# An attention and quantized-FFN kernel on one core: the last group of the up projection stays on chip for the down projection, and the general path becomes loops

## The chip, the cores and the metric

The kernel runs on one core of one Trainium2 chip. A core has TensorE (PE in the profile; its weight loads are PEld), VectorE (DVE), ScalarE (ACT), GpSimd (POOL) and SyncE (SP), which here issues almost all DMAs. The metric is the device time of one execution in microseconds, the median over several executions.

## The reference

The input x is (2, 2048, 512), ctx is (2, 128, 512). The kernel computes

```python
x = x + xattn(layernorm(x), ctx, Wq, Wkv)       # softmax attention, 128 keys
x = x + ffn(layernorm(x), w_gate, w_up, w_down) # 512 -> 1536 -> 512

def ffn(x, w_gate, w_up, w_down):
    x = act_qdq(x)
    up = act_qdq(x @ lpbq_dequant(w_up).T)
    gate = act_qdq(x @ lpbq_dequant(w_gate).T)
    sig = fixed_qdq_u16(sigmoid(gate))
    gate = act_qdq(gate * sig)
    o = act_qdq(gate * up)
    return o @ lpbq_dequant(w_down).T
```

`act_qdq` rounds a whole tensor to 16-bit integers with one scale, max|v| / 32767. `lpbq_dequant` rounds weights to 4 bits in blocks of 32. Every scale is a maximum over a whole tensor, so a stage can't round its result before all of it is known. The 16-bit integers are split into parts of at most 12 bits, and one product becomes three fp32r products: two summed in a PSUM tile q, the third in e.

## The kernel before

The 4096 tokens are 8 groups of 512. The 1536 features of the FFN are 12 chunks of 128, taken as 3 tiles of 4 chunks. The kernel has these stages in a row: attention and layernorm; gate (all groups, 0 to 7); up (groups 7 down to 0); down; the store of the last rows.

**Up** is the loop L688–742. For each of 24 (group, tile) pairs j and each of two halves (half tile c = 2j + h), `project` (L502–511) makes 24 matmuls into q and e. ACT evicts q (L709), DVE subtracts e (L710), SP stores the half tile of u to DRAM (`up_d`, L717). Beside this, `next_gelu` (L591–599) reads a gate tile j + 2 ahead (1 MB, `load_gate`, two buffers) and lets ACT make its integers gi, the sigmoid sig in a tile of its own, and its 16-bit integers sq. `integers_of_p` (L651–658) multiplies gi and sq on DVE to the integers p and stores them (`p_d`). `bound` (L660–664) lets ACT take |u| (L662) and DVE the maximum of |u| p (L663, `pumax`). `umax` collects the maxima of |u|. At the start of group 0, `load_step(0)` (L629, L638, L640) loads what the first step of down needs: p of 256 tokens as 6 DMAs of 128 KB, u as 6 DMAs of 256 KB, x1 as 512 KB; this is read from group 7, since down goes through groups 7 to 0. In group 0 each of the three tiles also issues the loads of four weight chunks of down without their third part (512 KB each, L738); the twelve third parts (256 KB each) follow at L742.

**Between up and down** the scale of o has to be found. `fetch_best` (L668–686) finds for each partition the half tile whose |u| p is greatest, makes a row index on DVE (L674) and lets POOL read that row of u and of p back from DRAM with indirect DMAs (L679). The last half tile isn't among them and is treated from SBUF. L745–751 make r_u, the reciprocal scale of u, over all partitions (with a transpose by TensorE). L757 rounds the last half tile and the fetched rows on ACT, L758 takes the maximum of the product on DVE, L763 the maximum over partitions on POOL. L818–821 make a flag that tells whether this maximum is sure to be the greatest; L823 reads the flag into a register of every engine, and L824 branches. If the flag is 0 a **general path** (L825–862) reads all gate, u and p tiles again; it is written out 24 + 24 times. It isn't entered with these inputs, and all engines jump over it.

**Down** (L865–895) has 16 steps of 256 tokens, each of two units of 128. A step loads the next step's p, u and x1 (`load_step`), rounds u on ACT (`round_up`, L776), and for each unit makes the parts of o (`round_o`: DVE L790, L791, L793, L795, ACT cast L792), 24 matmuls into q (L881), 12 into e (L885), and finishes with ACT (L889), POOL (L891), DVE (L893) and a store (L895). The first unit's parts are made in three pieces.

The order of instructions on each engine comes from the tile framework's scheduler, that of the source lines with priorities; every engine works its own list in order and waits by semaphores. SP issues its DMAs in its own order too, so one that waits holds the ones behind it.

Of the kernel before, what the change touches and what calls it, by code (L numbers as in the profile page):

```python
# [63 lines left out]
P = 128  # L64
# [12 lines left out]
def tile_xattn_ffn(  # L77
# [39 lines left out]
    x1_d = dram.tile([NG, P, NJ, D], F32, name="x1_d")  # L117
    gate_d = dram.tile([NG * NK, P, NQ, TG], F32, name="gate_d")

# [36 lines left out]

    def abs_max(col, src, axis=AX.X):
        nc.vector.tensor_reduce(col, src, axis, ALU.max, apply_absolute_value=True)
# [75 lines left out]
    cp = ExitStack()  # L234
    with ExitStack() as c0:
# [254 lines left out]
        homes = [cp.enter_context(tc.tile_pool(name="parts0", bufs=1))]  # L490
# [22 lines left out]
        with ExitStack() as c2:  # L513
# [16 lines left out]
            homes.append(home1.__enter__())  # L530
# [7 lines left out]
            for t in range(NG):  # L538
# [8 lines left out]
                for k in range(NK):  # L547
# [13 lines left out]
                    nc.sync.dma_start(out=gate_d[n], in_=g4)  # L561
# [4 lines left out]
    order = [(t, k) for t in reversed(range(NG)) for k in range(NK)]  # L566
    with cp, ExitStack() as c3:
        gp2 = c3.enter_context(tc.tile_pool(name="gate", bufs=2))
        wk1 = c3.enter_context(tc.tile_pool(name="wkc1", bufs=1))
        wk2 = c3.enter_context(tc.tile_pool(name="wkc2", bufs=2))  # L570
        wk3 = c3.enter_context(tc.tile_pool(name="wkc3", bufs=3))
# [7 lines left out]
        def load_gate(t, k, queue=nc.sync):  # L579
            gt = gp2.tile([P, NQ, TG], F32, tag="gt", name=f"gt_{t}_{k}")  # L580
            queue.dma_start(out=gt, in_=gate_d[t * NK + k])
            return gt

        gts = [load_gate(*at, nc.gpsimd) for at in order[:2]]
# [6 lines left out]
        def gelu_like(pool, pool1, gt, shape, name):  # L591

            gi = pool.tile([P] + shape, I16, tag="gi", name=f"gi_{name}")
            nc.scalar.activation(gi, gt, AF.Copy, scale=r_g)
            sig = pool1.tile([P] + shape, F32, tag="sig", name=f"sig_{name}")
            nc.scalar.activation(sig, gi, AF.Sigmoid, scale=s_g)
            sq = pool.tile([P] + shape, U16, tag="sq", name=f"sq_{name}")
            nc.scalar.activation(sq, sig, AF.Copy, scale=65536.0)  # L598
            return gi, sq


        gi, sq = gelu_like(const, const, top_g, [1], "top")
# [13 lines left out]
        wd, ready, loaded = [], [], {}  # L616

        lds = []

        def where_of(t):  # L620


            g, i = divmod(t * TD, TG)
            return g, NG - 1 - g, i

        def load_p(t, v):
            g, _, i = where_of(t)
            for c in range(2 * NK):
                nc.sync.dma_start(out=v[:, ts(c, 2), :], in_=p_d[g * 2 * NK + c, :, :, ds(i, TD)])  # L629

        def load_step(t):
            g, tg, i = where_of(t)
            pool = lds[t % 2]
            pi = pool.tile([P, NF, TD], I16, tag="p5", name=f"p5_{t}")
            load_p(t, pi)
            uv = pool.tile([P, NF, TD], F32, tag="u5", name=f"u5_{t}")
            for c in range(2 * NK):
                nc.sync.dma_start(out=uv[:, ts(c, 2), :], in_=up_d[g * 2 * NK + c, :, :, ds(i, TD)])  # L638
            x1 = pool.tile([P, TD // P, D], F32, tag="x1", name=f"x1_{t}")
            nc.sync.dma_start(out=x1, in_=x1_d[tg, :, ds(i // P, TD // P), :])  # L640
            loaded[t] = pi, uv, x1

        def next_gelu():

            j = len(ready)
            if j < len(order):
                ready.append(gelu_like(wk3, wk1, gts.pop(0), [NQ, TG], j))
                if j + 2 < len(order):
                    gts.append(load_gate(*order[j + 2]))

        def integers_of_p(j):  # L651
            gi, sq = ready[j]
            pi = wk3.tile([P, NQ, TG], I16, tag="pi", name=f"pi_{j}")
# [6 lines left out]
        def bound(c, u, pi):  # L660
            ua = wk2.tile([P, 2, TG], F32, tag="ua", name=f"ua_{c}")
            nc.scalar.activation(ua, u, AF.Abs)  # L662
            nc.vector.tensor_tensor_reduce(ua, ua, pi, 1.0, 0.0, ALU.mult, ALU.max, pumax[:, c : c + 1])  # L663
            return ua

        best = const.tile([P, 8], F32, name="best")

        def fetch_best():  # L668
# [5 lines left out]
            nc.vector.scalar_tensor_tensor(row, where[:, 0:1], float(P), lane, ALU.mult, ALU.add)  # L674
# [11 lines left out]
            return fetched  # L686

        LAST = len(order) - 1  # L688
        for j, (t, k) in enumerate(order):
            if k == 0:  # L690
# [3 lines left out]
                if t == 0:  # L694
                    home1.__exit__(None, None, None)
                    lds.append(ctx.enter_context(tc.tile_pool(name="ld0", bufs=1, side="right")))
                    load_step(0)
            u4 = wk2.tile([P, NQ, TG], F32, tag="u4", name=f"u4_{j}")
            if j:
                pi = integers_of_p(j)  # L700
            for h in range(2):
                c = 2 * j + h
                both = slice(2 * h, 2 * h + 2)
                q = ps_m.tile([P, 2, TG], F32, tag="q", name=f"q_u{c}")
                e = ps_m.tile([P, 2, TG], F32, tag="e", name=f"e_u{c}")
                for i in range(2):
                    project(wu[NQ * k + 2 * h + i], parts, q[:, i, :], e[:, i, :])
                if c + 1 < NH:
                    nc.scalar.activation(u4[:, both, :], q, AF.Copy, scale=1.0 + 1.0 / BASE)  # L709
                    nc.vector.tensor_tensor(u4[:, both, :], u4[:, both, :], e, ALU.subtract)  # L710
                else:
                    for i in range(2):
                        v = u_last[:, i, :]
# [205 lines left out]
```

## Time and profile before

| | us |
|---|---|
| median of 5 runs | 1027.84 (1023.53 to 1030.06) |
| the profiled execution | 1027.78 |
| its span in the profile | 1026.0 |

One execution was profiled, at a mean granted TensorE clock of 0.967. Of its span, PE is busy 951.1 us (93%), PEld 765.5 (75%), DVE 801.1 (78%), ACT 541.8 (53%), POOL 81.1 (8%). The page cuts the span in 40 slices of 25.65 us; digits are tenths of a slice in which the engine was busy:

```profile
PE   6998875999999999997999999999549999999998
PEclk9999896999999999999999999999869999999999
DMA  9087644886895775897789988896978876666520
```

The first eight slices are attention, then gate, up from slice 18 on, and down from slice 29 to the end. The two slices near the middle of the right half with 5 and 4 on PE are the transition from up to down. The row PEclk is the clock that TensorE was granted. Costliest on DVE in up are the subtraction of e (57.2 us), L663 (57.3) and L654 (56.4), in down L790 (61.2).

### The profile page before, as it was taken

Reading aid. Unit: us, or ns where it says so; the run is one execution under the profiler, and the core shown is the slowest. Engines: PE = TensorE matmul, PEld = TensorE weight load, DVE = VectorE, ACT = ScalarE, POOL = GpSimd, SP = SyncE. Lnnn points to the kernel's source line nnn. Section 1 sums busy time; section 2 is a strip of 40 time slices with the busy share of each in tenths; the row PEclk is TensorE's granted clock in tenths of the full one; section 3 lists DMA queues with packets and bytes.
Section 4 is the critical chain, followed back from the end, with each engine's and each line's share of the span. In section 5 each row is a group of like instructions: output and inputs, shape, how many; then the busy total and the mean of one; then the engine's idle time right before and its main releaser. Section 6 shows DMA issues by size and latency. Waiting matters only on the chain. (4 is left out here: it accounts for less than half of the span.)

```text
span 1026.0 us, 11754 instructions
## 1 busy us (share of the span) xinstructions
PE 951.1 (93%) x4321; PEld 765.5 (75%) x4321; DVE 801.1 (78%) x969; ACT 541.8 (53%) x610; POOL 81.1 (8%) x67
## 2 busy tenths in 40 slices
PE   6998875999999999997999999999549999999998
PEld 5765643888888888876888888888338888888886
DVE  4489865899997989445898888788558997877882
ACT  2268786432333323219998898886335344344431
POOL 0101111000000000000000000000001321122111
PEclk9999896999999999999999999999869999999999
DMA  9087644886895775897789988896978876666520
GB/s 337 18 320 273 246 180 172 325 335 273 322 376 187 301 228 176 272 391 290 288 320 376 346 314 326 341 359 222 415 243 264 277 241 202 222 207 200 175 74 31
DMA packets 127262, 268.47 MB, mean 262 GB/s; under 512 B 7456, under 2 KB 75040, under 8 KB 118496
## 3 DMA queue, kind: packets, MB, share of 16 engines
q1 hardware_dynamic: 126160, 263.75, 71.3%
q0 software_dynamic: 512, 2.88, 0.8%
q10 hardware_dynamic: 528, 1.05, 0.3%
q8 instruction: 34, 0.56, 0.2%
q14 instruction: 28, 0.23, 0.1%
HBM read 140.77 MB, written 126.88 MB: 261 GB/s over the span
## 5 line engine op out<-in xcount | busy, mean ns | idle before, releaser
L881 PE MATMUL yq<-wd,parts_o 128*128 128x512 f32 x768 | 181.9, 393 | 24.1 <-DMA p<-p_d 24.1
L507 PE MATMUL q_g<-parts_g,wg 128*128 128x512 f32 x768 | 196.0, 396 | 5.1 <-ACT parts_g L225 5.1
L881 PEld LDWEIGHTS yq<-wd,parts_o 128*128 128x128 f32 x768 | 145.8, 190 | 55.0 <-ACT parts_o L792 24.3
L507 PEld LDWEIGHTS q_g<-parts_g,wg 128*128 128x128 f32 x768 | 144.4, 189 | 38.1 <-ACT parts_g L225 6.2
L555 ACT ACTIVATE g<-q_g 128x512 f32<-128x512 f32 x96 | 57.3, 599 | 183.0 <-PE q_g L507 178.7
L507 PE MATMUL q_u<-parts_u,wu 128*128 128x512 f32 x576 | 144.2, 392 | 0.0
L507 PEld LDWEIGHTS q_u<-parts_u,wu 128*128 128x128 f32 x576 | 108.1, 188 | 24.4
L511 PE MATMUL e_g<-parts_g,wg 128*128 128x512 f32 x384 | 106.3, 395 | 0.0
L556 DVE CUSTOM_DVE_ANT_0 g<-g,e_g 128x512 f32<-128x512 f32 x96 | 64.6, 679 | 39.0 <-PE e_g L511 38.5
L885 PE MATMUL ye<-wd,parts_o 128*128 128x512 f32 x384 | 92.2, 389 | 0.0
L511 PEld LDWEIGHTS e_g<-parts_g,wg 128*128 128x128 f32 x384 | 72.2, 189 | 15.7
L885 PEld LDWEIGHTS ye<-wd,parts_o 128*128 128x128 f32 x384 | 72.1, 188 | 15.0
L511 PE MATMUL e_u<-parts_u,wu 128*128 128x512 f32 x288 | 77.9, 392 | 0.0
L889 ACT ACTIVATE yqs<-yq,q_o 128x512 f32<-128x512 f32 x32 | 22.0, 687 | 100.9 <-PE yq L881 100.9
L792 ACT CAST parts_o<-sa_o 128x1536 fp32r<-128x1536 int16 (+1 forms) x34 | 47.4, 1397 | 48.7 <-PE ye L885 26.3
L891 POOL TENSOR_TENSOR qx<-yqs,x 128x512 f32<-128x512 f32 x32 | 55.1, 1723 | 217.6 <-ACT yqs L889 205.3
L663 DVE CUSTOM_DVE_ANT_0 ua<-ua,pi 128x1024 f32<-128x1024 f32 x47 | 57.3, 1221 | 18.8 <-ACT ua L662 18.6
L654 DVE SCALAR_TENSOR_TENSOR pi<-gi,k_p,sq 128x2048 int16<-128x2048 int16 x24 | 56.4, 2350 | 16.9 <-ACT sq L598 16.1
L790 DVE SCALAR_TENSOR_TENSOR oi<-p,k_o,ui 128x1536 int16<-128x1536 int16 (+1 forms) x34 | 61.2, 1808 | 9.3 <-DVEq L824 5.9
L710 DVE TENSOR_TENSOR u<-u,e_u 128x1024 f32<-128x1024 f32 x47 | 57.2, 1217 | 8.6 <-ACT u L709 8.6
L511 PEld LDWEIGHTS e_u<-parts_u,wu 128*128 128x128 f32 x288 | 54.1, 188 | 12.2
L893 DVE SCALAR_TENSOR_TENSOR y<-ye,e_o,qx 128x512 f32<-128x512 f32 x32 | 24.0, 750 | 47.2 <-PE ye L885 37.9
(178 smaller groups left out, 1415.8 us busy)
## 6 DMA issues: line engine op xcount, KB each, us to landing
gate_d<-g SPq DMA_DIRECT2D x24, 1024.0 KB, 6.5
u<-up_d SPq DMA_DIRECT2D x96, 256.0 KB, 4.7
up_d<-u SPq DMA_DIRECT2D x47, 512.0 KB, 6.3
gt<-gate_d SPq DMA_DIRECT2D x22, 1024.0 KB, 7.9
parts_d<-parts_g SPq DMA_DIRECT2D x6, 3072.0 KB, 11.4
parts_u<-parts_d SPq DMA_DIRECT2D x6, 3072.0 KB, 12.4
p_d<-pi SPq DMA_DIRECT2D x24, 512.0 KB, 9.7
p<-p_d SPq DMA_DIRECT2D x96, 128.0 KB, 2.9
```

Of the source, the lines that this page charges most:

```text
L507: nc.tensor.matmul(q, lhsT=w[:, s, c, :], rhs=parts[:, s, c, :], start=(c + s == 0), stop=(c + s == ND))
L511: nc.tensor.matmul(e, lhsT=w[:, 2, c, :], rhs=parts[:, 2, c, :], start=(c == 0), stop=(c == ND - 1))
L555: nc.scalar.activation(g4[:, i, :], q, AF.Copy, scale=1.0 + 1.0 / BASE)
L556: nc.vector.tensor_tensor_reduce(g4[:, i, :], g4[:, i, :], e, 1.0, LOWEST, ALU.subtract, ALU.max, gtop[:, m : m + 1])
L654: nc.vector.scalar_tensor_tensor(pi, gi, k_p, sq, ALU.mult, ALU.mult)
L663: nc.vector.tensor_tensor_reduce(ua, ua, pi, 1.0, 0.0, ALU.mult, ALU.max, pumax[:, c : c + 1])
L710: nc.vector.tensor_tensor(u4[:, both, :], u4[:, both, :], e, ALU.subtract)
L790: nc.vector.scalar_tensor_tensor(oi[:, c], pi[:, c], k_o, ui[:, c], ALU.mult, ALU.mult)
L792: nc.scalar.copy(parts[:, 0, c], a[:, c])
L881: nc.tensor.matmul(q, lhsT=parts[:, s, f, :], rhs=wd[f][:, s, :], start=(f + s == 0), stop=(f + s == NF))
L885: nc.tensor.matmul(e, lhsT=parts[:, 2, f, :], rhs=wd[f][:, 2, :], start=(f == 0), stop=(f == NF - 1))
L891: nc.gpsimd.tensor_tensor(qx, qs, x1[:, j, :], ALU.add)
```

## The change

1. A pool `keep` of three buffers holds u tiles and p tiles of group 0 past the end of up. Down goes through group 0 first, from these tiles, and then groups 7 to 1.
2. The pools in which the parts of h stood (`parts0`, `parts1`) stay to the end. At the start of group 0 the first four weight chunks of down, all three parts, 768 KB each, are loaded into the buffer where group 1's parts were; `load_step(0)` is gone. The other eight chunks follow behind the first and the second tile of group 0 (two parts) and behind the last store of u (third part).
3. The parts of o go to the other of these buffers and to three late weight buffers. `oi` and `sa` are single tiles.
4. `load_up` reads u for a whole group as three 1 MB DMAs (rows of 4 KB) in place of 6 x 256 KB for each 256 tokens. p and x1 still come step by step.
5. `gelu_like` lets the sigmoid write over the gate tile. `gate_d` is stored in the order in which up reads it.
6. The last half tile goes to two pairs of PSUM tiles; the order of its evictions against `bound` and the row index is fixed by `in_order`, which adds an order of issue and no wait. r_u takes fewer steps on DVE. ui of the first step is rounded in three pieces on ACT (`round_up`), each behind a given instruction.
7. Both loops of the general path are `For_i` loops of 24 rounds.
8. In the first four units `round_o` works in pieces of four chunks, in a fixed order. The result y is written into qx. The first x1 is loaded behind the branch.

```diff
-        def gelu_like(pool, pool1, gt, shape, name):
+        def gelu_like(pool, gt, shape, name):
+            sq = pool.tile([P] + shape, U16, tag="sq", name=f"sq_{name}")
             gi = pool.tile([P] + shape, I16, tag="gi", name=f"gi_{name}")
             nc.scalar.activation(gi, gt, AF.Copy, scale=r_g)
-            sig = pool1.tile([P] + shape, F32, tag="sig", name=f"sig_{name}")
-            nc.scalar.activation(sig, gi, AF.Sigmoid, scale=s_g)
-            sq = pool.tile([P] + shape, U16, tag="sq", name=f"sq_{name}")
-            nc.scalar.activation(sq, sig, AF.Copy, scale=65536.0)
+            nc.scalar.activation(gt, gi, AF.Sigmoid, scale=s_g)
+            nc.scalar.activation(sq, gt, AF.Copy, scale=65536.0)
             return gi, sq
...
-            pi = wk3.tile([P, NQ, TG], I16, tag="pi", name=f"pi_{j}")
+            pi = keep.tile([P, NQ, TG], I16, tag="pi", name=f"pi_{j}")
+            kept_p.append(pi)
...
+        def load_down(fs, part=slice(None)):
+            loads = []
+            for f in fs:
+                if f == len(wd):
+                    wd.append(first_wd[:, f] if f < NE else chunk_tile([P, 3, D], "wd", f - NE))
+                loads.append(nc.sync.dma_start(out=wd[f][:, part, :].bitcast(F32), in_=wd_d[f, :, part, :]))
+            return loads
...
-                    home1.__exit__(None, None, None)
-                    lds.append(ctx.enter_context(tc.tile_pool(name="ld0", bufs=1, side="right")))
-                    load_step(0)
-            u4 = wk2.tile([P, NQ, TG], F32, tag="u4", name=f"u4_{j}")
+                    first_wd = homes[1].tile([P, 3, ND, TG], F32R, tag="parts", name="first_wd")
+                    first_wd = first_wd.rearrange("p s c (k d) -> p (s c k d)", k=1).rearrange(
+                        "p (f s d) -> p f s d", f=NE, s=3
+                    )
+                    load_down(range(NE))
+            u4 = keep.tile([P, NQ, TG], F32, tag="u4", name=f"u4_{j}")
...
                     for i in range(2):
-                        v = u_last[:, i, :]
-                        nc.scalar.activation(v, q[:, i, :], AF.Copy, scale=1.0 + 1.0 / BASE)
-                        nc.vector.tensor_tensor(v, v, e[:, i, :], ALU.subtract)
+                        v = u4[:, 2 + i, :]
+                        q = ps_m.tile([P, 2, TG], F32, tag="q", name=f"q_u{c}_{i}")[:, 0, :]
+                        e = ps_m.tile([P, 2, TG], F32, tag="e", name=f"e_u{c}_{i}")[:, 0, :]
+                        project(wu2[i], parts, q, e)
+                        in_order(magnitudes, nc.scalar.activation(v, q, AF.Copy, scale=1.0 + 1.0 / BASE))
+                        in_order(to_row, nc.vector.tensor_tensor(v, v, e, ALU.subtract))
                         abs_max(umax[:, LAST + 1 + i : LAST + 2 + i], v)
-                nc.sync.dma_start(out=up_d[c], in_=u4[:, both, :] if c + 1 < NH else u_last)
...
-            if t == 0:
-                for f in range(NQ * k, NQ * (k + 1)):
-                    w = chunk_tile([P, 3, D], "wd", f)
-                    nc.sync.dma_start(out=w[:, :2, :].bitcast(F32), in_=wd_d[f, :, :2, :])
-                    wd.append(w)
-        for f in range(NF):
-            nc.sync.dma_start(out=wd[f][:, 2, :].bitcast(F32), in_=wd_d[f, :, 2, :])
+            if t == 0 and k + 1 < NK:
+                load_down(range(NE + NQ * k, NE + NQ * (k + 1)), slice(0, 2))
+        in_order(stored, *load_down(range(NE, NF), slice(2, 3)))
...
+        NS = TG // TD
+        groups = [0, *reversed(range(1, NG))]
...
+        def load_up(g):
+            tiles = []
+            for k in range(NK):
+                u4 = keep.tile([P, NQ, TG], F32, tag="u4", name=f"u5_{g}_{k}")
+                nc.sync.dma_start(
+                    out=u4.rearrange("p (h c) t -> p h c t", h=2), in_=up_d[rows_of(g, k)].rearrange("h p c t -> p h c t")
+                )
+                tiles.append(u4)
+            return tiles
...
+        def round_up(t, tiles, places=()):
+            ui = wki.tile([P, NF, TD], I16, tag="ui5", name=f"ui5_{t}")
+            for k in range(NK):
+                made = nc.scalar.activation(
+                    ui[:, ts(k, NQ), :], tiles[k][:, :, ts(t % NS, TD)], AF.Copy, scale=r_u
+                )
+                in_order(*places[k : k + 1], made)
+            return ui
+        a_home = homes[0].tile([P, 3, ND, TG], F32R, tag="parts", name="o_parts").rearrange("p s c t -> p (s c t)")
+        b_home = [wp_late.tile([P, 3, D], F32R, tag="wp", name=f"o_parts{i}") for i in range(3)]
+        o_parts = [
+            [a_home[:, ts(i, NF * P)].rearrange("p (f k) -> p f k", k=P) for i in range(3)],
+            [v.rearrange("p s (c k) -> p (s c) k", k=P) for v in b_home],
+        ]
+        oi, sa = (wki.tile([P, NF, P], I16, tag=tag, bufs=1, name=tag) for tag in ("oi", "sa"))
...
+        uis = {0: round_up(0, tiles_u, rounded)}
...
+                with tc.For_i(0, NG * NK, 1) as j:
+                    gi, sq, v = gate_integers(j, "a")
+                    nc.vector.scalar_tensor_tensor(v, gi, s_g16, sq, ALU.mult, ALU.mult)
+                    keep_max(pmax, v, "p")
...
-        lds.append(c5.enter_context(tc.tile_pool(name="ld1", bufs=1)))
...
+        ld = c5.enter_context(tc.tile_pool(name="ld", bufs=2))
+        units = range(TD // P)
+        pieces = [ts(k, NQ) for k in range(NK)]
+        p5, x1s = {}, {0: load_x1(0)}
         for t in range(NT // TD):
             if t + 1 < NT // TD:
-                load_step(t + 1)
-            pi, uv, x1 = loaded.pop(t)
-            ui = up_tile(t) if t else ui_first
-            if t:
-                round_up(ui, uv, r_u)
-            else:
-                round_up(ui[:, :, P:], uv[:, :, P:], r_late)
-            for j in range(TD // P):
-                m = t * (TD // P) + j
-                parts = round_o(o_tiles(m), pi[:, :, ts(j, P)], ui[:, :, ts(j, P)], 1 if m else 3)
-                q = ps_y.tile([P, D], F32, tag="q", name=f"yq_{m}")
-                e = ps_y.tile([P, D], F32, tag="e", name=f"ye_{m}")
-                for f in range(NF):
-                    for s in range(2):
-                        nc.tensor.matmul(
-                            q, lhsT=parts[:, s, f, :], rhs=wd[f][:, s, :], start=(f + s == 0), stop=(f + s == NF)
-                        )
-                for f in range(NF):
-                    nc.tensor.matmul(
-                        e, lhsT=parts[:, 2, f, :], rhs=wd[f][:, 2, :], start=(f == 0), stop=(f == NF - 1)
-                    )
-                qs = wk2.tile([P, D], F32, tag="qs", name=f"yqs_{m}")
-                nc.scalar.activation(qs, q, AF.Copy, scale=q_o)
-                qx = wk2.tile([P, D], F32, tag="qx", name=f"qx_{m}")
-                nc.gpsimd.tensor_tensor(qx, qs, x1[:, j, :], ALU.add)
-                y = wk2.tile([P, D], F32, tag="y", name=f"y_{m}")
-                nc.vector.scalar_tensor_tensor(y, e, e_o, qx, ALU.mult, ALU.add)
-                _, g, i = where_of(t)
-                nc.sync.dma_start(out=of[ds(g * TG + i + j * P, P), :], in_=y)
+                x1s[t + 1] = load_x1(t + 1)
+                if t + 1 >= NS:
+                    p5[t + 1] = load_p(t + 1)
+            ui, x1 = uis.pop(t), x1s.pop(t)
+            for j in units:
+                m, w = t * len(units) + j, ts(j, P)
+                parts = o_parts[m % 2]
+                if t < NS:
+                    at = ds(t * TD + j * P, P)
+                    made = [round_o(parts, kept_p[k][:, :, at], ui[:, c, w], c) for k, c in enumerate(pieces)]
+                    in_order(*chain(*made), *[third_part(parts, c) for c in pieces])
+                else:
+                    round_o(parts, p5[t][:, :, w], ui[:, :, w])
+                    third_part(parts)
+                q, e = first_sum(m, parts), second_sum(m, parts)
+                if j == 0 and t + 1 < NT // TD:
+                    uis[t + 1] = round_up(t + 1, tiles_u)
+                    if t % NS == NS - 2 and t + NS < NT // TD:
+                        tiles_u = load_up(groups[t // NS + 1])
+                finish(t, j, q, e, x1)
 # ---- launch: one core; inputs and outputs as the reference has them ----
```

## Prediction

> **What bounds the kernel now.** I read the page's busy shares and its chain first, then the busy times by stage, then the waits, the timeline and the transfers of the one stretch in which TensorE does nothing. In the stage table the columns behind the stretch are its length, then the busy time of PE, PEld, DVE, ACT and POOL, the granted clock, the DMA share and GB/s.
>
> ```profile
> 457.69:486.00 28.31, 22.90 (x96) 17.83 (x96) 15.69 (x24) 21.80 (x18) 0.37 (x1) 1.00 0.80 299
> 486.00:730.74 244.74, 244.65 (x1056) 199.24 (x1056) 208.47 (x184) 207.03 (x155) 0.00 (x0) 0.99 0.87 326
> 730.74:758.07 27.33, 0.30 (x3) 0.14 (x2) 10.05 (x32) 6.22 (x7) 2.45 (x3) 0.60 0.82 315
> 758.07:1022.03 263.96, 263.94 (x1152) 217.82 (x1152) 210.66 (x163) 109.09 (x80) 55.15 (x32) 0.99 0.62 195
> ```
>
> Up (second row) and down (fourth) are TensorE without a gap. Between them lie 27.33 us with 0.30 us of TensorE. So the change can gain in that gap, in the 5.4 us that up loses while it starts (first row), and nowhere else: the matmuls of both stages stay the same 1152 and 1152. It can lose wherever the cover of a stage is broken. The waits of 730 to 759 us, and the timeline of the same stretch (start, duration, engine, line), name the gap's links:
>
> ```profile
> PE yq L881 <- DMA p<-p_d: 24.1, 1, 24.1
> ACT ui_b L757 <- DMA best<-up_d,row: 8.0, 1, 8.0
> DVE oi L790 <- DVEq L824: 5.9, 1, 5.9
> ```
> ```profile
> 738.63 1.08 POOL L679 DMA_INDIRECT best<-up_d,row  x1 [277.95 <-DMA wd<-wd_d]
> 745.79 1.15 ACT L757 ACTIVATE ui_b<-best,r_u 128x1024 int16<-128x1024 f32 x1 [7.96 <-DMA best<-up_d,row]
> 748.91 0.22 DVE L821 SCALAR_TENSOR_TENSOR flag<-top,floor,a_o 128x1 int32<-128x1 f32 x1
> 755.70 1.41 DVE L790 SCALAR_TENSOR_TENSOR oi<-p,k_o,ui 128x512 int16<-128x512 int16 x2 [5.92 <-DVEq L824]
> 757.40 1.14 ACT L792 CAST parts_o<-sa_o 128x512 fp32r<-128x512 int16 x2 [7.38 <-DVE sa_o L791]
> 758.07 8.18 PE L881 MATMUL yq<-wd,parts_o 128*128 128x512 f32 x24 [24.09 <-DMA p<-p_d]
> ```
>
> Backwards: the first product of down waits for a cast (757.40), that for DVE, which stood still after the branch of L824. The name "p" at the first wait is the semaphore that came last by the profile; p5 had landed at 707.90, so it is not the cause. The branch waits for the flag (748.91), that for the best tile's rounding (745.79), that for the indirect load issued at 738.63. The load reads up_d, so it waits for the store of half tile 46: issued at 727.84, landed at 737.57 in the trace. The row index was ready at 729.91, so the store sets this. The chain is: **store 9.73, issue 1.06, load 7.16, rounding to branch 4.46 (745.79 to 750.25), branch to first product 7.82**.
>
> **The change, part by part.**
>
> **Store of half tile 46.** The two stretches of the stage table that tell why it takes 9.73 us:
>
> ```profile
> 702.25:714.50 12.25, 12.25 (x56) 10.14 (x55) 9.79 (x9) 8.60 (x8) 0.00 (x0) 1.00 0.88 258
> 714.50:737.60 23.10, 16.54 (x73) 13.26 (x71) 17.46 (x31) 9.70 (x11) 0.00 (x0) 0.96 1.03 417
> ```
>
> While down's first step is loaded (L697: 6 x 128 KB in rows of 512 bytes, 6 x 256 KB in rows of 1 KB, 512 KB of x1) the queues move 258 GB/s, after it 417, and they stay full. The last of that load lands at 717.59; behind it the fifteen transfers of 512 KB up to the store land one every 1.26 us or so (the last at 737.57). The change drops these reads (group 0's u and p stay in SBUF) and puts four chunks of 768 KB in their place: 3.1 MB at 417 GB/s is 7.5 us from 702, done at about 710 and landed at 712. The fifteen then land as they are issued. By the issue times of before (709.75 for the first, 721.86 to 723.87 for the last four weight chunks) and 1.26 us each, the queue is served up to 727.7 when the store comes at 727.84, with the p store (726.33) before it: 730.2 at its end, and some 2 us of landing (the lightly loaded store of 695.03 took 2.60): 732.2, which is 5.4 earlier. Bounds: 0 (the chunks are served as slowly as the small pieces) and 7.1 (2.60 us landing). I take 5.4. Issue 1.06 and load 7.16 I leave: the rest behind the store still fills the queue, with 2 MB of third parts (5 MB of weights were issued behind it before). [...] The rounding then begins at 740.4; r_u is there at 735.19, so nothing new is late.
>
> **Rounding to branch.** The same five steps, 4.46 us: branch on DVE at 744.9. The product's own tile takes no copy. ACT now rounds three pieces of ui behind the best tile (L813–820 of the changed kernel) at 1.05 each by the 128x1024 row of L662: it ends about 744.7, then loads the flag and branches at 745.2, beside DVE.
>
> **Branch to first product, 7.82 us.** Jump to next instruction in the trace, against the rows of the general path jumped over in the program's order: PE 0 rows 0.30 us, POOL 2 rows 0.41, ACT 168 rows 2.96, SP 148 rows 3.2, DVE 133 rows 5.26. The transfers of 749 to 757 us show what was waited for:
>
> ```profile
> q14 instruction: 7, 0.06, 2.2%
> ```
>
> Seven fetches of code of 8 KB. On the page that queue has 28 fetches and 0.23 MB in all, for 1,973 rows executed on DVE, ACT, POOL and SP: 117 bytes a row, so one fetch holds about 70 rows (an estimate). With the loops the general path is 40 rows on DVE, 29 on SP, 21 on ACT, 16 on POOL, 15 on PE: less than one fetch, so the target lies in the block at hand or the next. Bounds: 0.3 (PE's row) and 5.26 (DVE's). I take 0.4, POOL's row, the nearest in length. Saved: 4.9.
>
> [...]
>
> Behind the jump before needed 2.37 us to the first product (755.70 to 758.07): two oi pieces went ahead of the first cast. The change writes the order oi 0.75, sa 0.29, cast 0.62, and ACT still has one ui piece of 1.05 to do behind its own branch, beside DVE. DVE starts 745.2, the cast follows at 746.3, the product at about 747.2, taking 0.3 for semaphores. **So 758.07 becomes 747.2: 10.9 less** (5.4 store, 4.9 code, 0.6 order).
>
> **Start of up.** Sigmoid now writes into the gate tile, which frees it only after sq, and in the program's order ACT does gi, gi, sig, sig, sq, sq before the second half tile is evicted. Before had two stalls of PE (1.99 at 476.69, 3.44 at 486.02); now there is one of about 6 us at 474 to 480 and one near 1.4. The set of ACT work ahead of half tile 4's eviction is the same, so this ends alike: bounds -0.4 and +2.2, I take +0.3.
>
> **Later gate loads.** The next gate load is issued some 5.6 us later each time (gi to end of sq, 506.26 to 511.16 and beyond). Its cover before: load of j6 landed 513.86 and gi began 513.89 (0 us), the others of the stage 2 to 11 us. ACT works 207.03 of 244.74 us there and can catch up 37.7, PE stands two half tiles behind. I cost it 0 and say below what it is without cover.
>
> **Down.** Per unit PE needs 5.44 + 2.72 = 8.16 us, DVE 210.66 / 32 = 6.6, ACT 3.4, POOL 1.7: bound by PE as before. u loaded by 3 x 1 MB in rows of 4 KB per group replaces 12 x 256 KB; needed about 12 us after issue for the first group, 29 for the later ones; 1 MB gate loads landed in 5.8 to 13.6 us, so the first group is the thin place (0 to +2). First 768 KB chunks are complete with the third part. x1_0 is loaded only after the branch: 512 KB, needed some 9 us later. Taken 0.
>
> **First unit.** Its q takes 8.18 in place of 5.44 because the granted clock was 0.50 from 735.95 to 763.25, until 5.2 us into down. The gap still is 16.5 us, over three times the 5.2 us after which the clock fell, so I keep that loss: 2.7 ± 1.
>
> **Sum** against the profiled execution: 1027.78 - 10.9 + 0.3 = **1017.2 us**. That execution lies 0.06 under the median of the five runs (1027.84), so the same number stands for the median. About 0.5% (5.1 us) is what a measurement of this kernel can tell from no change: 1022.7 and 1033 are the bounds.
>
> **Rivals.**
> 1. The code fetch stays (5.26 in place of 0.4, or 2.96 of ACT): 1027.78 - 6.0 + 0.3 = 1022.1. For it: seven fetches followed the jump whatever the engine's row count, and the loops' branches may send the fetcher elsewhere. Against: POOL and PE at 0.3 to 0.4.
> 2. The change doesn't shorten the store: the 768 KB chunks meet the same backlog, or the indirect load takes 7.16 plus what the store gained. Saved 5.5 alone: 1022.6. For it: the DMA share is 0.9 to 1.03 throughout. Against: 258 against 417 GB/s for the two kinds of load.
> [...]
> 4. Slower: gate tiles late. If each load lands 5.6 later against covers of 2.3, 0, 2.1, 4.0, 4.3, 3.3 and 3.9 (the third tile of seven groups), ACT stands 19.3 us; it is in order, so evictions of q and then PE stand too. Uncovered that is 1017.2 + 19.3 = 1036.5. It decides from 15.8 us of PE stall, 2.3 a group. For it: j6 had no cover. Against: ACT idles 37.7 us in the stage, and most of those loads stand behind 3 MB of parts in the queue, so landing shifts by less than issue (about 2.5).
>
> **Chances:** forecast 0.57, rival 1 0.13, rival 2 0.12, rival 3 0.11, rival 4 0.07 (5 points of it over 1033, 2 of it between). Rivals 1 and 2 fall half under 1022.7 and half above. So faster 0.57 + 0.11 + 0.13 = 0.81, same 0.12 + 0.02 = 0.14, slower 0.05. The range holds forecast, 1 and 2 and the near part of 3: 1012.5 to 1023.5.
>
> **What would show it.** Right: last product of up at 731 ± 1; store of half tile 46 landed within 5 us of issue; rounding of the best tile at 740; DVE's gap behind the branch under 0.6 us and no fetch in it; first product of down at 747; 32 units of 8.16. Wrong: an indirect load above 8 us, code fetches behind the branch, PE gaps in up every third tile ahead of an eviction, or PE gaps at the first casts of a group in down.

## The result, and the profile after

The changed kernel takes **1027.83 us** (median of 37 runs, 1025.16 to 1030.85) against 1026.68 (67 runs, 1023.53 to 1032.21): a ratio of **1.0009** with a 95% interval of 1.0002 to 1.0016. A gain of 10.6 us was forecast, and there is none. The profiled execution took 1028.76 us, its span is 1027.0.

The stage table of the changed kernel, cut at the first and last matmul of up and of down, has the columns of the prediction's table (length, busy time of PE, PEld, DVE, ACT and POOL, granted clock, DMA share, GB/s):

```profile
457.95:486.00 28.05, 25.16 (x107) 20.02 (x108) 16.83 (x25) 23.34 (x18) 0.37 (x1) 1.00 0.73 284
486.00:729.11 243.11, 240.54 (x1047) 195.78 (x1045) 207.44 (x185) 205.93 (x155) 0.00 (x0) 1.00 0.87 331
729.11:751.58 22.47, 0.44 (x2) 0.13 (x1) 9.17 (x30) 7.23 (x8) 2.43 (x3) 0.58 0.62 238
751.58:1022.72 271.14, 270.38 (x1152) 216.93 (x1152) 215.19 (x188) 112.70 (x115) 44.30 (x32) 0.99 0.55 183
```

Compare by length: up 271.2 (272.9 before, measured in the same way), the gap 22.5 (27.5), and **down 271.1 against 263.8**. The gap gave 5.0 us and up 1.7; down took 7.3 back. PE is still busy nearly all the time in down (270.38 of 271.14 us), for the same 1152 matmuls: its share hides the loss, and only the stage's length shows it. The page's chain that ended last says that down has changed its nature. Before, it was a row of L881 and L885 on PE (26% of the span). Now it is

```profile
issue 15%; PE 4%; DVE 4%; POOL 2%; DMA 1%; ACT 1%; SPq 0%; POOLq 0%; DVEq 0%; ACTq 0%
```

PE has lost its place. Most of the chain is "issue", time in which an engine waited for nothing that the profile shows, so the page doesn't name a cause. The timeline gives the beats. These are the first rows of units 19 to 22 (a unit is 128 tokens, counted from 0):

```profile
911.36 2.03 PE L851 MATMUL yq<-first_wd,o_parts 128*128 128x512 f32 x8
919.64 2.19 PE L851 MATMUL yq<-first_wd,o_parts 128*128 128x512 f32 x8
928.43 2.13 PE L851 MATMUL yq<-first_wd,o_parts 128*128 128x512 f32 x8 [0.19 <-ACT o_parts L838]
936.92 2.19 PE L851 MATMUL yq<-first_wd,o_parts 128*128 128x512 f32 x8
```

From 762.31 to 919.64 nineteen units take 8.28 us each; from there to 1014.26 eleven take 8.60 in the mean. Before, it was 8.16 from the second unit on (8.25 once). So 19 x 0.12 + 11 x 0.44 + 0.2 (the last unit and that 8.25) = 7.3: two causes, a small one in every unit and a larger one in the last third.

The gap in the timeline of the changed kernel:

```profile
736.98 1.07 POOL L670 DMA_INDIRECT best<-up_d,row  x1 [276.04 <-DMA wd<-wd_d]
744.08 1.15 ACT L764 ACTIVATE ui_b<-best,r_u 128x1024 int16<-128x1024 f32 x1 [10.45 <-DMA best<-up_d,row]
747.20 0.22 DVE L897 SCALAR_TENSOR_TENSOR flag<-top,floor,a_o 128x1 int32<-128x1 f32 x1
749.21 0.75 DVE L835 SCALAR_TENSOR_TENSOR oi<-pi,k_o,ui 128x512 int16<-128x512 int16 x1 [1.16 <-DVEq L900]
750.93 0.60 ACT L838 CAST o_parts<-sa 128x512 fp32r<-128x512 int16 x1
751.58 3.78 PE L851 MATMUL yq<-first_wd,o_parts 128*128 128x512 f32 x8 [19.91 <-ACT o_parts L838]
```

DVE's wait behind the branch fell from 5.92 to 1.16: the loops did what they should. The indirect load starts only 1.65 us earlier, which is what up gained: the store of half tile 46 was issued at 726.10 and landed at 736.04, 9.94 us against 9.73.

### The profile page after: what moved, and what is told of

Read it like the earlier page. It is cut to its first block, busy times and chain, and to the rows that moved or that the text cites. A ratio compares the mean times of both kernels' runs of the same rounds, so it can differ in the third digit from the quotient of the medians.

```text
span 1027.0 us, 11691 instructions
## 1 busy us (share of the span) xinstructions
PE 955.8 (93%) x4321; PEld 763.1 (74%) x4321; DVE 805.2 (78%) x996; ACT 546.7 (53%) x647; POOL 70.2 (7%) x67
## 5 line engine op out<-in xcount | busy, mean ns | idle before, releaser
L851 PE MATMUL yq<-wd,o_parts 128*128 128x512 f32 x512 | 122.7, 392 | 0.0
L851 PEld LDWEIGHTS yq<-wd,o_parts 128*128 128x128 f32 x512 | 96.9, 189 | 21.4
L838 ACT CAST o_parts<-sa 128x1536 fp32r<-128x1536 int16 (+1 forms) x40 | 48.6, 1215 | 85.1 <-DVE sa L836 85.1
L816 ACT ACTIVATE ui<-u,r_u 128x1024 int16<-128x1024 f32 x48 | 53.3, 1142 | 68.1 <-DVE oi L835 66.5
L851 PE MATMUL yq<-first_wd,o_parts 128*128 128x512 f32 x256 | 68.5, 410 | 20.7 <-ACT o_parts L838 20.7
L851 PEld LDWEIGHTS yq<-first_wd,o_parts 128*128 128x128 f32 x256 | 48.0, 192 | 36.2 <-ACT o_parts L838 25.0
L859 PE MATMUL ye<-wd,o_parts 128*128 128x512 f32 x256 | 63.9, 391 | 0.0
L868 DVE SCALAR_TENSOR_TENSOR qx<-ye,e_o,qx 128x512 f32<-128x512 f32 x32 | 24.0, 749 | 47.8 <-POOL qx L867 40.5
L839 DVE SCALAR_TENSOR_TENSOR o_parts<-sa,oi 128x1536 fp32r<-128x1536 int16 (+1 forms) x40 | 57.5, 1438 | 3.5 <-DVE sa L836 0.5
```

The source lines that it names most:

```text
L816: made = nc.scalar.activation(ui[:, ts(k, NQ), :], tiles[k][:, :, ts(t % NS, TD)], AF.Copy, scale=r_u)
L838: nc.scalar.copy(parts[0][:, c], sa[:, c])
L839: made.append(nc.vector.scalar_tensor_tensor(parts[1][:, c], sa[:, c], -BASE, oi[:, c], ALU.mult, ALU.add))
L851: nc.tensor.matmul(q, lhsT=parts[s][:, f, :], rhs=wd[f][:, s, :], start=(f + s == 0), stop=(f + s == NF))
L859: nc.tensor.matmul(e, lhsT=parts[2][:, f, :], rhs=wd[f][:, 2, :], start=(f == 0), stop=(f == NF - 1))
```

## The experiments

"Ratio" is against the kernel before, with its 95% interval; the medians are of 5 to 12 runs. Line numbers are those of each kernel. Times of stages are from one profiled execution each, and up varies from 269.0 to 274.5 us among them, with the stalls at its start and the clock there.

### e1: the cast behind the eviction

```diff
+            cast = nc.scalar.copy(parts[0][:, c], sa[:, c])
+            in_order(*evicted[-2:-1], cast)
...
+            evicted.append(nc.scalar.activation(qs, q, AF.Copy, scale=q_o))
```

> The changed kernel with one order added: on ACT the cast of unit m+2 stands behind the eviction of q of unit m. In the changed kernel it stands ahead of it, and from 919 us on a unit takes 8.60 us in place of 8.28. Theory 1 (a ring: DVE finishes a unit, makes the third part, then oi and sa of the next, ACT casts, then evicts q, POOL adds x1, DVE finishes; one unit per turn, 8.6 us): with the eviction first the ring is open, units take 8.28 us to the end, the last unit begins some 3.6 us earlier, about 1024. Rival 1 (DVE's or POOL's own load, or the reads of u by tiles, sets the last third): units stay at 8.6 there, about 1027.8.

1025.35 us, ratio 0.9975 (0.9961 to 0.9990); the profiled execution, 1022.07, is the fastest of the twelve. Units take 8.28 to the end (two near its start 8.61 and 8.44) and down 267.2 in place of 271.1. Theory 1 holds. The ring, in one turn of the changed kernel's timeline:

```profile
938.84 0.75 DVE L868 SCALAR_TENSOR_TENSOR qx<-ye,e_o,qx 128x512 f32<-128x512 f32 x1 [1.68 <-POOL qx L867]
939.51 1.75 DVE L843 SCALAR_TENSOR_TENSOR o_parts<-sa,oi 128x1536 fp32r<-128x1536 int16 x1
941.29 1.82 DVE L835 SCALAR_TENSOR_TENSOR oi<-p,k_o,ui 128x1536 int16<-128x1536 int16 x1
943.22 0.56 DVE L836 TENSOR_SCALAR sa<-oi 128x1536 int16<-128x1536 int16 x1
944.20 1.46 ACT L838 CAST o_parts<-sa 128x1536 fp32r<-128x1536 int16 x1
945.57 0.68 ACT L865 ACTIVATE yqs<-yq,q_o 128x512 f32<-128x512 f32 x1
945.72 2.23 PE L851 MATMUL yq<-first_wd,o_parts 128*128 128x512 f32 x8 [0.20 <-ACT o_parts L838]
946.32 1.30 POOL L867 TENSOR_TENSOR qx<-yqs,x 128x512 f32<-128x512 f32 x1 [7.51 <-ACT yqs L865]
947.66 0.75 DVE L868 SCALAR_TENSOR_TENSOR qx<-ye,e_o,qx 128x512 f32<-128x512 f32 x1 [1.67 <-POOL qx L867]
```

Read it as a circle. DVE's finish of one unit (938.84) stands in DVE's queue ahead of the third part, oi and sa; ACT casts the sa and only then evicts q (945.57), though that q, of unit 21, had been ready since 934.07; POOL adds x1, and DVE's next finish (947.66) can start. This turn takes 8.82 us, the next 8.48 (a piece of ui ahead of the cast makes the difference). None of these three is busy for 8 us of it: DVE waits 1.7 for POOL, ACT 5.7 for DVE, POOL 7.5 for ACT. PE itself is not in the ring. It starts a unit when the cast is done, and the casts have a lead over it that shrinks by some 0.3 us a unit: 4.5 us for unit 8, 0.27 for unit 19, 0.06 for unit 20. That is why the beat changes only at 919.64. In the kernel before, the cast of unit m+2 came behind the eviction of q of unit m, in the program's order. There the three parts of a unit were one tile, so that cast had to wait for e of unit m; now part 0 is a tile of its own and free when q of unit m is done, and the scheduler put the cast first. That this is why it did so is argued, not tried; that the order costs the time is shown.

### e2: the first four weight chunks not read

```diff
-                        q, lhsT=parts[s][:, f, :], rhs=wd[f][:, s, :], start=(f + s == 0), stop=(f + s == NF)
+                        q, lhsT=parts[s][:, f, :], rhs=wd[max(f, NE)][:, s, :], start=(f + s == 0), stop=(f + s == NF)
```

> As the kernel with the cast behind the eviction, and the matmuls of chunks 0 to 3 of down read the weights of chunk 4 instead (that part of the computation is changed); the first four chunks are still loaded. In the changed kernel a matmul of these chunks takes 233 ns and the others 227. Theory 2 (the place in SBUF from which the first four chunks are read, the buffer where odd groups' parts stood, costs 6 ns a matmul, as for the odd groups in up of the kernel before): every matmul 227 ns, units 8.16 us, about 3.7 us less than the kernel with the cast behind alone, about 1020.5. Rival 2 (it is the switch between tiles or the parts' buffers, not the place read): units stay at 8.28.

1022.13 us, ratio 0.9947 (0.9930 to 0.9963). Units take 8.16 us and down 264.0 (three units near its start waited 1.4 us in sum). Theory 2 holds: the 0.12 us a unit come with reading these chunks from that buffer. The time lies 5 us above the forecast of the whole change, though both losses of down are undone in it.

### e3: the loops alone

```diff
-                for j in range(NG * NK):
-                    gi, sq = tile_of_gate(j, "a")
+                with tc.For_i(0, NG * NK, 1) as j:
+                    gi, sq, v = gate_integers(j, "a")
```

> The kernel before with the general path as two loops, nothing else (the gate tiles are stored by the order of up so that the loops can index them). Theory 3 (the jump over the written-out path costs the fetch of code): DVE's wait behind the branch falls from 5.9 us to some 1.2, the first product of down comes 4.5 to 5 us earlier, all of it reaches the end: about 4.7 below the kernel before, 1022. Rival 3 (the gain of the gap belongs to the other parts of the change): no change, or the third parts of the weights land too late and take it back.

1028.42 us, ratio 1.0013 (1.0000 to 1.0027): no gain. DVE's wait behind the branch is 1.23 us and the gap 22.3 in place of 27.5, so theory 3 is right about the jump, and rival 3 about the time. The waits of 755 to 790 us in this kernel show what took it back:

```profile
DVE oi L790 <- DMA p<-p_d: 4.5, 1, 4.5
ACT ui L776 <- DMA u<-up_d: 4.5, 1, 4.5
PE yq L886 <- ACT parts_o L792: 2.9, 1, 2.9
```

The reads of step 1 are issued behind the branch and SP's wait for the third weight parts, at 756.25 us (755.60 in the kernel before). PE reached unit 2 at 773.9 and had to wait until 776.92, where the kernel before began it at 776.96, and unit 3 was 2.05 late as well. The loops are worth their 5 us only with tiles of u and p at hand for the first two steps. The kept tiles give just that: in the changed kernel units 2 and 3 follow without a stall. The wait itself isn't the same in every run with the written-out path: the profiles of e8 and e12, below, have 3.93 and 4.18 us of it, and there too PE begins units 2 and 3 late, by 4.0 us in sum, so that the shorter wait didn't reach the end of down.

### e4: chunks 8 to 11 behind the last store

```diff
-            if t == 0 and k + 1 < NK:
-                load_down(range(NE + NQ * k, NE + NQ * (k + 1)), slice(0, 2))
-        in_order(stored, *load_down(range(NE, NF), slice(2, 3)))
+            if t == 0 and k == 0:
+                load_down(range(NE, 2 * NE), slice(0, 2))
+        in_order(stored, *load_down(range(2 * NE, NF)), *load_down(range(NE, 2 * NE), slice(2, 3)))
```

> The changed kernel with the loads of weight chunks 8 to 11 (two parts, 2 MB) moved from behind the second tile of group 0 to behind the last store of u, there with all three parts. Theory 4 (the store of half tile 46 waits its turn behind the bytes issued ahead of it in a full queue, 9.9 us from issue to landing): 2 MB less at 412 GB/s is 5.1 us less, it lands about 5 us after issue, the indirect load starts near 732 and the rounding of the best tile near 739.5; first product of down 4 to 5 us earlier, total about 1023.5. Rival 4 (the indirect load then meets the moved bytes and takes as much longer): rounding stays near 744, total 1027.8.

1026.66 us, ratio 0.9992 (0.9979 to 1.0005). The store of half tile 46 landed 4.71 us after its issue, as theory 4 has it. The indirect load took 8.67 in place of 7.07, so the flag came 3.5 us earlier, counted from the end of up. But the gap shrank by 1.4 alone: ACT now had six pieces of ui (744.83 to 751.17) ahead of the first cast, which DVE had ready at 748.6. The edit that freed one link loaded the next one.

### e5: a spacer of 192 bytes

```diff
+            spacer = ctx.enter_context(tc.tile_pool(name="spacer", bufs=1, side="right"))
+            nc.vector.memset(spacer.tile([P, 48], F32, name="spacer"), 0.0)
             home1 = tc.tile_pool(name="parts1", bufs=1, side="right")
```

> The kernel with the cast behind the eviction, and a spacer of 192 bytes a partition ahead of the buffer of the odd groups' parts, so that this buffer and with it the first four weight chunks begin 192 bytes lower (at an offset of 288 in 512 bytes, as the buffer of the even groups does). Theory 2a (the 6 ns a matmul come from where the rows begin within a block of some hundred bytes): all matmuls of down 227 ns, and those of the odd groups of up as well; units 8.16 us; 3.7 us less in down and 4 groups x 144 matmuls x 6 ns = 3.5 us less in up than the kernel with the cast behind, about 1018. Rival 2a (they come from the part of SBUF, the highest 24 KB, whatever the offset): 233 ns stay, 1025.4.

**1017.14 us, ratio 0.9904 (0.9881 to 0.9928)**, 8.2 below the same kernel without the spacer. Eight matmuls of q in the timeline of the changed kernel, from the start of one row to the next:

```profile
828.55 2.03 PE L851 MATMUL yq<-first_wd,o_parts 128*128 128x512 f32 x8
830.42 3.81 PE L851 MATMUL yq<-wd,o_parts 128*128 128x512 f32 x16
```

and in that of this kernel:

```profile
831.83 1.98 PE L856 MATMUL yq<-first_wd,o_parts 128*128 128x512 f32 x8
833.65 3.79 PE L856 MATMUL yq<-wd,o_parts 128*128 128x512 f32 x16
```

1.87 us for eight are 233 ns each, 1.82 are 227. Up's odd groups fell from 233.3 to 226.7 too. The matmuls that read the four chunks are not the whole 0.12 us of a unit: by the starts of the rows they lose 0.05 in q and 0.03 in e, and the matmuls of the other chunks behind them, which begin at equal offsets, 0.02 each time. With the spacer all of it is gone.

### e6 and e7: the first ui early, then with the late chunks

```diff
+            if t:
+                ui = wki.tile([P, NF, TD], I16, tag="ui5", name=f"ui5_{t}")
+            else:
+                ui = wp_late.tile([P, 3, D], F32, tag="wp", name="ui5_0").bitcast(I16)
...
-        uis = {0: round_up(0, tiles_u, rounded)}
+        uis = {0: round_up(0, tiles_u, rounded[:1])}
```

> The kernel with the cast behind the eviction, and the rounded u of down's first step goes to a weight buffer that is free after up, its three pieces behind the rounding of the last half tile. In the changed kernel its buffer lies where the best tile's integers stood, so the first piece waits for DVE's product (746.41) though r_u is there at 732.4. Theory 5 (these pieces stand in ACT's queue ahead of the first cast and hold it 0.65 us): the pieces run near 734 to 737, the cast follows sa at once, the gap from the last matmul of up to the first of down shrinks from 21.7 to about 21.0, total 0.7 less, 1024.7. Rival 5 (the cast waits for something else): no change.

1024.13 us, ratio 0.9975 (0.9962 to 0.9988); the gap is 20.5 in place of 21.7. The pieces held the cast, as theory 5 has it: from the flag to the first product it is 3.79 us in place of 4.39. The other half of the gain lies ahead of the flag (the store landed 0.4 us sooner after its issue, the indirect load took 0.2 less), where nothing was changed.

> The same with chunks 8 to 11 loaded behind the last store of u. In the changed kernel with that edit alone the store landed 4.7 us after its issue and the flag came 3.5 us earlier measured from the end of up, but ACT then had six pieces of ui to do ahead of the first cast (746 to 751) and the gap shrank by 1.4 alone. Theory 6 (the early store is worth 3.5 us once ACT is free): gap about 18.3, total 2.5 to 3.5 less than the kernel with the early ui, about 1021.5. Rival 6 (the longer indirect load or the late chunks take it back): gap 20 or more, or the first unit's matmuls wait for chunk 8.

1023.84 us, ratio 0.9971 (0.9955 to 0.9987). This one didn't test theory 6: with the loads moved, all six pieces of ui came behind the best tile's rounding again in ACT's order (741.97 to 748.32), and the gap was 21.1. Fixing a piece behind one instruction doesn't put it ahead of another.

### e8: the spacer in the kernel before

> The kernel before with the spacer of 192 bytes alone, so that the odd groups' parts begin at another offset. Theory 2a (the offset within a block costs 6 ns a matmul): the 4 x 144 matmuls of the odd groups in up 227 ns in place of 233, 3.5 us, and some 2 us in the odd groups of the gate stage; down is unchanged, since it reads its weights elsewhere; about 1021 against 1026.7. Rival 2b (the gain of the spacer came from something it does to the end of the changed kernel alone): 1026.7.

1027.66 us, ratio 1.0003 (0.9991 to 1.0016): a miss. The odd groups' matmuls stay at 233.3 ns although their rows now begin at 288. Theory 2a falls: the offset of the rows alone doesn't decide.

### e9: the spacer in the changed kernel

> The changed kernel with the spacer alone, the cast left ahead of the eviction. Theories 1 and 2a together (the ring sets 8.6 us a unit as soon as PE's lead is used up, and PE's own unit falls to 8.16): the gate and up stages gain some 5.5 us, in down the units start at 8.16, the change to 8.6 comes earlier (the lead is lost at 0.44 a unit in place of 0.32, so after some 14 units) and the end of down is the same distance from its start, about 1022. Rival 1 (no ring): units 8.16 to the end, 1017.

1023.57 us, ratio 0.9958 (0.9942 to 0.9973). Down takes 271.2, no less than without the spacer: units of 8.2 up to about 880, of 8.6 behind it. PE was faster and the ring just began to pace it sooner. The gain is that of gate and up. So the order of the cast alone is worth 2.5 us (e1), the spacer alone 4.3, both together 10.7 (e5): each loss in down hid part of the other.

### e10 and e11: all together

```diff
+                ui_first = wp_late.tile([P, 3, D], F32, tag="wp", name="ui5_0").bitcast(I16)
...
+                    made = nc.scalar.activation(ui_first[:, ts(k, NQ), :], v[:, :, :TD], AF.Copy, scale=r_u)
+                    in_order(rounded[-1], made)
+                    rounded.append(made)
+            else:
+                in_order(*rounded[-2:])
```

> The spacer, the cast behind the eviction, and ui of the first step early in the free weight buffer, its pieces fixed behind the last half tile's rounding and ahead of the best tile's, the second step's pieces behind the first unit's casts. Against the kernel with spacer and cast order (1017.1): the gap 1.2 us shorter as with the early ui before, 1016.

1016.33 us, ratio 0.9892 (0.9875 to 0.9908); the gap is 21.3, that of e5 22.0.

> The same with chunks 8 to 11 behind the last store of u. With ACT's queue free behind the branch theory 6 (the early store is worth 3.5 us) gives a gap of about 17 to 18 and some 3 us less than without it, 1013. Rival 6 (the longer indirect load, above all that of p, takes it back): 1016.

**1012.36 us, ratio 0.9851 (0.9836 to 0.9866)**: the fastest of all, and faster than both kernels. Its stages:

```profile
455.79:726.80 271.01, 264.22 (x1152) 217.72 (x1152) 224.03 (x210) 229.37 (x172) 0.37 (x1) 0.99 0.86 327
726.80:746.00 19.20, 0.44 (x2) 0.13 (x2) 8.64 (x30) 8.32 (x8) 2.43 (x3) 0.58 0.84 309
746.00:1010.47 264.47, 263.72 (x1152) 217.50 (x1152) 228.03 (x188) 113.11 (x114) 51.27 (x32) 0.99 0.56 187
```

The early store is worth 4.0 us in the median against e10, 2.1 in the gaps of the two profiles (the profiled execution of e11, 1016.28 us, is the slowest of its five). The gap is longer than forecast: the two indirect loads took 8.75 and 9.00 us (7.18 and 6.99 in e10), and DVE's product waits for the second.

### e12 and e13: equal and unequal offsets

```diff
-            nc.vector.memset(spacer.tile([P, 48], F32, name="spacer"), 0.0)
+            nc.vector.memset(spacer.tile([P, 32], F32, name="spacer"), 0.0)
```

> The kernel before with a spacer of 128 bytes in place of 192. Theory 2c (a matmul is 6 ns longer when the rows that it streams and the weights that it was loaded with begin at different offsets in 512 bytes): in the kernel before weights and even groups begin at 352, the odd groups at 480; 192 bytes made that 288, different still, and changed nothing; 128 bytes make it 352, so the odd groups' matmuls take 227 ns in up and gate, about 5.5 us less, 1021.5. Rival 2d (the changed kernel profits from the offset 288 as such, or from something else that the spacer does to it): 233 ns and 1027 stay.

1021.18 us, ratio 0.9944 (0.9926 to 0.9961): the matmuls of up's odd groups take 226.7 ns like the others. The kernel before gains 5.6 us from 128 bytes, and gained none from 192.

> The changed kernel with the cast behind the eviction and a spacer of 128 bytes: the weights, the parts of o and the even groups begin at 288, the odd groups and the first four weight chunks at 352 (480 without a spacer, 288 with the one of 192 bytes). Theory 2c: 233 ns stay for the odd groups and the first four chunks, units of 8.28 us, about 1025. Rival 2e (only the offset 480, the last 32 bytes of a block of 512, is slow): 227 ns, units of 8.16 and 1017.

1020.67 us, ratio 0.9938 (0.9921 to 0.9955). In between: up's odd groups at 229.0 ns, the first four chunks in down at 231.9, units of down 8.26. Both theories miss here in size. Unequal offsets cost, as theory 2c says, but 64 bytes above the weights cost 2.3 ns in up, and 64 below them (e8) 6.6.

## Why the prediction was wrong, step by step

**Where the time is.** Right for the kernel before: TensorE bounds up and down (busy 244.65 of 244.74 us and 263.94 of 263.96), and the gap can be shortened (27.5 us to 22.5). Wrong that there is nothing to gain elsewhere: e12 takes 5.6 us from the same matmuls.

**Store of half tile 46.** Wrong: 5.4 us were forecast and none came. The four chunks were loaded at 339 GB/s (701.76 to 714.49), not at the 417 taken from the later stretch, and their end was 3.1 us earlier than that of the old loads, not 5.6. In the 14 us from 701 the queues moved 4.5 MB (3.4 before), and from 715 to the landing they ran full in both (DMA share 1.03, 412 and 417 GB/s). The transfers from there to the store took 20.2 us from the first landing to the last, 18.6 before, so by landings the store gained 1.5 us, and its issue was 1.7 earlier. The extra 1.6 us lie in one place: between 719.56 and 722.19 one transfer of 512 KB landed while 1.03 MB moved, so part of what moved belonged to transfers behind it. From 722.19 to the store's landing they land one every 1.26 us, about as before (1.25). Why the queue did so is not shown. Only the runs that take 2 MB out of the way (e4, e7, e11) shortened the landing, to 4.71, 4.64 and 5.66. So rival 2 came true, whose price was 1022.6. Rival 3 (1013, 0.11 of the chances) came from an estimate of mine of how short the indirect load can get, and no run shows it: the load took 6.7 to 8.8 us.

**Rounding to branch.** Right: 4.38 (744.08 to 748.46) against 4.46.

**Jump.** Right: the wait fell by 4.8 us (e3: 4.7) for a forecast of 4.9, though three code fetches still follow the branch (q14, 749.1 to 750.0) and 1.16 us are left where under 0.6 was to show it. The trace has 3,035 rows on the four engines, those for semaphores and branches included, not 1,973, so a fetch of 8 KB holds some 108 rows (an estimate); the loops' 40 are still less.

**Order behind the branch.** Wrong by a little: 3.1 us from DVE's branch to the first product for 2.3 forecast, in part because ACT began its ui pieces late (their buffer lay where the best tile's integers were read until 746.41; the cast stood behind the fourth, 0.65 us after its input was ready). The rest is the jump, 0.75 us from DVE's branch to its next instruction for 0.4 forecast. e6 took 0.6 us of it back. The 0.3 us taken for semaphores was an estimate of mine that no run shows; in e11 0.09 us passed from the end of sa to the cast (745.24 to 745.33) and 0.05 from the cast's end to the product (745.95 to 746.00).

**Start of up.** Outside its bounds of -0.4 to +2.2, to the good: up was 1.7 shorter. PE's two stalls are 5.8 us in sum in both kernels; but before, the clock was 0.62 in the mean from 486.02 to 490.46, after, 1.00 through the start. That wasn't forecast, so these 1.7 us are luck.

**Later gate loads, first unit.** Right: PE has no stall in up behind 492 us, and the first unit still takes 10.73 us.

**Down.** This is the step that failed: "bound by PE as before ... Taken 0", and it cost 7.3 us. Two things were missing in it.
- I compared PE's 8.16 us with the *sum* of work of each other engine. None is over 6.8 us. But in-order queues can close a ring across engines in which each waits for the next, and its turn is a sum along the ring (8.6 us here), whatever the loads are. The order in which ACT held cast and eviction stood in the changed program and could have been read. Price: 3.7 us (11 units x 0.32 and 0.17 in the last, by the beats; e1 in down: 3.9, with a first unit 0.7 shorter and two others 0.5 longer in sum).
- I took a matmul to be 227 ns wherever its operand lies. The trace of the kernel before contradicted it: in up the odd groups had 233.3 ns in the mean and the even ones 226.7. The rows below are of an even group and then of an odd one; the eight matmuls of q take 1.81 and 1.87 us from row to row. The change puts a third of down's weights in the odd groups' buffer. Price: 31 x 0.12 = 3.7 us (e2 against e1 in down: 3.2).

```profile
568.17 1.98 PE L507 MATMUL q_u<-parts_u,wu 128*128 128x512 f32 x8
569.98 1.07 PE L511 MATMUL e_u<-parts_u,wu 128*128 128x512 f32 x4
600.88 2.03 PE L507 MATMUL q_u<-parts_u,wu 128*128 128x512 f32 x8
602.75 1.10 PE L511 MATMUL e_u<-parts_u,wu 128*128 128x512 f32 x4
```

Of the rivals, none named either; the one on the slower side, late gate tiles, did not happen. With down 7.3 us shorter the median would be 1020.5 (an estimate); e2, in which both losses of down are undone, took 1022.13. Both are inside the range, in its upper part, and 3 to 5 us above the forecast, where the store's 5.4 are missing. That e5 measured 1017.14, next to the forecast of 1017.2, is chance: its spacer also shortens gate and up, which the prediction didn't have.

In sum, for the profiled execution (1028.76 us, forecast 1017.2): the store 5.6, the order behind the branch 0.8 and down 7.3 us more than forecast, up 2.0 and the steps between 0.3 less; that is 11.4 of the 11.6.

## What to carry to other kernels

When a change makes buffers free earlier or splits a tile, write down the order on each in-order queue for one turn of the loop and follow the circle; its sum is a bound like an engine's load (here 8.6 us a unit, where PE alone needed 8.28). When a gap shrinks and the end stays, measure each later stage from its own start: the loss here was in the beat of a stage whose bounding engine looked just as busy. And a matmul's operands have a place as well as a shape (here 226.7 or 233.3 ns for the same shape): compare the distance of starts between buffers before moving an operand.

## What the runs showed of the hardware

Distance of matmul starts (128x128 weights, 128x512 rows, fp32r), by the offset in 512 bytes at which weights and rows begin in the compiled programs:

| weights | rows | ns | where |
|---|---|---|---|
| 352 | 352 | 226.7 | kernel before, even groups; e12 |
| 352 | 480 | 233.3 | kernel before, odd groups |
| 352 | 288 | 233.3 | e8, odd groups |
| 288 | 288 | 226.7 | changed kernel, even groups; e5 |
| 288 | 480 | 233.3 | changed kernel, odd groups and first four chunks of down |
| 288 | 352 | 229.0 | e13, odd groups |
| 288 | 352 | 231.9 | e13, first four chunks of down |

Equal offsets were the fast case each time, but for the few matmuls directly behind unequal ones (see e5). Whether 512 bytes is the period that counts no run tests, nor which part of the chip makes the difference. The difference is 2.9% at most (233.3 against 226.7 ns).

The indirect load of the best tile took 6.7 to 7.2 us where 2 MB of weights were issued behind the last stores of u, and 8.7 to 8.8 where it was 4 MB (e4, e7, e11). The bytes alone don't set it: in the kernel before it was 5 MB, and the load took 7.1.
